# Four stacked layers on one core: index loads for two windows at once, an earlier reciprocal, later pieces of sample 1, and a column difference on VectorE

## The chip, the cores and the metric

The kernel runs on one core of a Trainium2 chip. The time is device microseconds (us) of one execution, the median of the runs shown. The engines are named as the profile names them: PE (TensorE's matmuls; PEld its weight loads), DVE (VectorE), ACT (ScalarE), POOL (GpSimd) and SP (SyncE, which here only issues DMAs). PSUM is the memory that matmuls write; SBUF is the one that the other engines work in.

## What is computed

A batch `x` of 8 samples, 128 channels, 56 x 56 pixels, float32, goes through four residual layers; each adds its result to a group-normalised input's branch:

```python
x = x + L0(_gn(x))   # windowed attention: 7x7 windows of 8x8 pixels, each attends to the 4 windows
                     # with the largest logits of window means; plus a depthwise 3x3 on v, then W_o
x = x + L1(_gn(x))   # batch norm, a tanhshrink projection, a recurrent net over 3136 pixels, projection
x = x + L2(_gn(x))   # a masked 3x3 convolution and a masked 1x1
x = x + L3(_gn(x))   # conv3x3, bn, relu, conv3x3, bn, + residual, relu
```

The part of layer 0 that matters here, and layer 3:

```python
logit = einsum('npc,nqc->npq', q_win * SCALE, k_win)
topk_logit, r_idx = top_k(logit, 4)
kv_sel = vmap(lambda kvn, idx: kvn[idx])(kv_pix, r_idx)          # 4 windows of keys and values
attn = softmax(einsum('bmqc,bmkc->bmqk', q_h * SCALE, k_sel))    # 8 heads
o = einsum('bmqk,bmkc->bmqc', attn, v_sel)

out = relu(bn1(conv3x3(x, w1)))
out = relu(bn2(conv3x3(out, w2)) + residual)
```

## The kernel before

X stays in SBUF. The order of PE, ACT, DVE and POOL in layers 0 and 3 is the order in which the program text issues them (`manual_schedule`); SP's queue runs in its own order of issue. Waits are put in between engines where data needs them.

**Layer 0** handles 8 x 49 windows as 196 pairs. In the loop over `p`, the pair `p + 1` gets its scores, row maxima (DVE, `nmax`), exponentials with their sums (ACT, `e`, `den`) and half its transposes, while the pair `p` finishes: second half of the transposes, copies to SBUF (`eT`, DVE and ACT in turn), the products with the values (`po`), the division. The names in the strings `SHORT` and `LONGER` (L762 to L765) are the order of one turn of the loop.

- `gather(W)` (L467): POOL reads the 4 indices of a window into registers (`chosen`, L457, a register load of four numbers at L460), copies the four key windows (L474, `ks`) and masks the queries (L476, `qm`). It is called two pairs ahead, from `ahead(p)` (L767).
- `fetch(W)` (L482): SP reads the same 4 indices into its own registers and issues 4 DMAs (L487, 32 KB each) of value windows from `vpix` in DRAM into `vs`, of which six buffers rotate, one per window.
- `divisors(p)` (L521): a DVE reciprocal of the exponentials' sums (L524, `rden`) and two POOL multiplications that spread it (L527, `rc`); `turn_divisors` transposes `rc` on PE (L556, `po`) in the next turn, ahead of the products with the values in PE's queue (L566).
- `light` is a small statistics or routing job (a matmul and its small follow-up): `mean`, `var`, `means`, `route`, once per sample. The follow-up of `var` (L235, samples 1 to 7) is three DVE operations and then twelve small POOL operations in a row (L246 to L249, three rounds of Newton's method for an inverse root).
- The work of later samples (normalising, keys, image rows, pixel rows, queries, depthwise, projection) is cut into pieces with a turn from which each is ready and one by which it is due; a planner (from L715 on) gives each turn up to two pieces and one light job. For sample 1 the statistics are due by turns 0 and 1, and the pieces of normalising stand at turns 2, 4, 6, 8, 10, 12, 15.

**Layer 1** (about 1345 to 2870 us) and **layer 2** (to about 3068 us) aren't touched.

**Layer 3** is two 3x3 convolutions of each sample, each as four blocks of 14 rows. Six column combinations per block (`column_sums`, L1403) go into the padded inputs `va` (first convolution) and `vb` (second), PE multiplies (`products`, L1440), and DVE combines (`outputs`, L1451). A `column_sums` has three parts: `outer` (two subtractions: `ce`, L1415, and `fg`, L1416, both on POOL save for two early `ce`), `inner` (DVE: `ab`, L1420; its sum and difference at L1421 and L1422 on DVE for `vb`, on POOL for `va`), and `ends` (DVE: L1426 to L1428, which read `ce` and `fg`). `block` puts these between its own steps: `outer` of the block before comes right after the copy on ACT, `inner` for `vb` just before the last operation of `outputs` (L1464), and for `va` behind it, after the two residual operations (L1558, L1559); `ends` follow. Thus POOL's queue holds, per block of the first convolution, `ce`, `fg`; and per block of the second one, `ce`, `fg` and then the sum and difference of `va`.

Of the kernel before, what the change touches and what calls it, by code (L numbers as in the profile page):

```python
# [10 lines left out]
F32 = mybir.dt.float32  # L11
# [3 lines left out]
ALU = mybir.AluOpType  # L15
# [3 lines left out]
P = 128  # L19
# [3 lines left out]
NW = 7  # L23
WS = 8
NWIN = NW * NW
WPX = WS * WS
# [18 lines left out]
def conv_stack_kernel(ctx: ExitStack, tc: tile.TileContext, a: dict, out: bass.AP):  # L45
# [80 lines left out]
    with ExitStack() as l0:  # L126
# [329 lines left out]

        def chosen(W, engine):  # L457

            b, w = divmod(W, NWIN)
            _, idx = nc.values_load_multi_w_load_instructions(  # L460
                selrs[b][0:1, w * TOPK : (w + 1) * TOPK], engines=[engine],
                min_val=0, max_val=NWIN - 1,
                skip_runtime_bounds_check_because="indices of maxima over 49 values, clamped to 48",
            )
            return idx

        def gather(W):  # L467


            b, w = divmod(W, NWIN)  # L470
            i, j = divmod(w, NW)
            kw = win.tile([P, TOPK, WPX], F32, name=f"ks_{W}", tag="ks")
            for t, at in enumerate(chosen(W, mybir.EngineType.Pool)):
                nc.gpsimd.tensor_copy(kw[:, t : t + 1, :], ks[b][:, bass.ds(at, 1), :])  # L474
            qm = win.tile([P, 2, WPX], F32, name=f"qm_{W}", tag="qm")
            nc.gpsimd.tensor_tensor(  # L476
                qm, qs[b, i][:, j : j + 1, :].broadcast_to((P, 2, WPX)),
                hmask.rearrange("p (h o) -> p h o", o=1).broadcast_to((P, 2, WPX)), ALU.mult,
            )
            wins[W] = dict(kw=kw.rearrange("p t x -> p (t x)"), qm=qm)  # L480

        def fetch(W):  # L482

            vw = wins[W]["vw"] = win.tile([P, 2, P], F32, name=f"vs_{W}", tag="vs", bufs=6)
            for t, at in enumerate(chosen(W, mybir.EngineType.SP)):
                h = (t % 2) * WPX
                nc.sync.dma_start(  # L487
                    vw[h : h + WPX, t // 2, :],
                    vpix[W // NWIN % 2][bass.ds(at, 1)].rearrange("o x c -> (o x) c"),
                )  # L490

        def scores(p):

# [194 lines left out]
        for b in range(1, B):  # L688

            at = [FIRST + 1] * NBLK if b == 1 else [pair_of(b - 2, 0) + i for i in range(NBLK)]  # L690
            if b > 1:
                for i in range(NBLK):
                    hook(max(at[i] - 8, FIRST + i // 2), lambda b=b, i=i: load_x(b, i, i + 1, nc.gpsimd))
            for i in range(4 * (b == 1), NBLK):
                hook(at[i], lambda b=b, i=i: once(measure, b)[0](i))
            job(at[-1] + 1, at[-1] + (1 if b == 1 else 5), lambda b=b: once(measure, b)[1], False, LIGHT, ("mean", b))
            job(at[-1] + 2, at[-1] + (2 if b == 1 else 9), lambda b=b: once(measure, b)[2], False, LIGHT,
                ("var", b), [("mean", b)])

            at = [pair_of(b - 1, i * NW) - 6 for i in range(NBLK)]  # L700
            if b == 1:
                at = [max(t, 2 + 2 * i) for i, t in enumerate(at)]
            due = pair_of(b, 0) - 3
            for i in range(NBLK):
                hook(at[i], lambda b=b, i=i: once(preparation, b)[0](i))
                job(at[i] + 1, due, lambda b=b, i=i: once(preparation, b)[1][i])
                job(at[i] + 1, due if i < 2 else pair_of(b, i * NW) - 10,
                    lambda b=b, i=i: once(preparation, b)[2][i], True)
                job(at[min(i + 1, NBLK - 1)] + 1, due - 1, lambda b=b, i=i: once(preparation, b)[3][i])
            job(at[-1] + 1, due - 2, lambda b=b: once(preparation, b)[4], False, LIGHT, ("means", b))  # L710
            job(at[-1] + 2, due - 1, lambda b=b: once(preparation, b)[5], False, LIGHT, None, [("means", b)])
# [43 lines left out]
        for k, (name, n) in enumerate(VECTORS):  # L755
# [4 lines left out]


        SHORT = """scores gather turn1 max0 max1 one turned old0 max2 exp00 exp01 old1 exp10 values end1 exp11 max3  # L762
            two exp02 exp03 exp12 exp13 hooks turn0 spread new1 end2 new0 tails light divisors divide"""
        LONGER = """scores gather turn1 max0 max1 exp00 old1 one end1 max2 max3 exp01 two old0 values turned exp02
            exp03 exp10 exp11 exp12 exp13 hooks turn0 spread new1 end2 new0 tails light divisors divide"""  # L765

        def ahead(p):  # L767
            if p + 2 < END:
                for W in (2 * p + 4, 2 * p + 5):
                    gather(W)  # L770
                for W in (2 * p + 4, 2 * p + 5) if p > FIRST + 1 else ():
                    fetch(W)
            for f in later:
                f()
            later.clear()
            for W in (2 * p - 2, 2 * p - 1):
                b, w = divmod(W, NWIN)
                if 0 <= b < B and w % NW == NW - 1:
                    join(b, w // NW)
# [13 lines left out]
        for p in range(FIRST, END + 6):  # L793
            now, then = 0 <= p < END, 0 <= p + 1 < END
            one, two, light = (t and t[3]() for t in plan[p])
            E, O = 2 * p + 2, 2 * p + 1
            acts = {
                "gather": lambda: ahead(p), "hooks": lambda: every(hooks.get(p, ())), "tails": rest,
            }
            if then:  # L800
                acts.update(scores=lambda: scores(p + 1), divisors=lambda: divisors(p + 1), turn0=lambda: turn(E),
                            new0=lambda: turned(E, 0), new1=lambda: turned(E, 1))
                for g in range(4):
                    acts[f"max{g}"] = lambda g=g: maxima(p + 1, g)
# [12 lines left out]
            for name in (LONGER if plan[p][1] and (not plan[p][0] or plan[p][1][5] == LONG) else SHORT).split():  # L817
                if name in acts:
                    acts[name]()
            for W in range(4) if p == FIRST + 1 else ():  # L820
                fetch(W)
        for f in later:
            f()
# [249 lines left out]
    def convolutions(held=None):  # L1073

        with ExitStack() as l2:
# [327 lines left out]
            def column_sums(v, lo, img, name, last=nc.vector, quick=False):  # L1403

                n = img.shape[2]
                at = [v[:, k].rearrange("p y x -> p (y x)")[:, lo * H4 : lo * H4 + n] for k in range(6)]
                ab, ce, fg = (
                    blk.tile([P, 2, size], F32, name=f"{k}_{name}", tag=k, bufs=2 - (k == "ab"))[:, :, :n]
                    for k in ("ab", "ce", "fg")
                )  # L1410
                other = nc.vector if quick else nc.gpsimd

                def outer():

                    other.tensor_tensor(ce, img[:, 3:5], img[:, 1:3], ALU.subtract)  # L1415
                    nc.gpsimd.tensor_tensor(fg, img[:, 0:4:3], img[:, 2:6:3], ALU.subtract)  # L1416

                def inner():

                    nc.vector.scalar_tensor_tensor(ab, img[:, 1:3], -4.0, img[:, 3:5], ALU.mult, ALU.add)  # L1420
# [395 lines left out]
```

## Time and profile before

| what | us |
|---|---|
| median of three runs (lowest, highest) | 3516.68 (3515.09, 3519.86) |
| the profiled execution's own time | 3514.11 |
| its span, first to last instruction | 3512.3 |
| PE busy in the span | 3396.8 (97%) |
| DVE, ACT, POOL busy | 1943.8, 1772.1, 1399.9 |
| layer 0, last products with values | ends at about 1337 |
| layer 3, first matmul to end of span | 3070.9 to 3512.3 |

The busy shares are averages over four layers with different limits. In layer 0 and layer 3 the waits of PE and the order of the queues of SP, DVE and POOL say more than the shares. TensorE's clock is granted in full nearly all the time; the profile records it as 0.992 over the span, and the stretches at one half are short (3.41 us or a multiple).

### The profile page before, as it was taken

The page shows a single profiled execution, that of the slowest core. Times are in us where ns is not written, and L with a number is a line of the kernel's source. Part 1 is how long each engine was busy: PE and PEld are TensorE (multiplying, and loading weights), DVE is VectorE, ACT ScalarE, POOL GpSimd, SP SyncE. Part 2 cuts the span into 40 slices and gives each one's busy share as a digit, 9 for nine tenths or more (in the row PEclk, how much of TensorE's full clock was granted, in tenths as well). Part 3 has the DMA queues.
Part 4 walks back from the last instruction along what each step waited for, and adds up shares of the span by engine and source line. Part 5 has one row for each costly group of instructions (what it writes and reads, how often), then busy time and mean ns, then how long its engine had stood idle before and what let it go on. Part 6 is the DMA issues. An engine that isn't in the chain of part 4 may idle for free.

```text
span 3512.3 us, 87799 instructions
## 1 busy us (share of the span) xinstructions
PE 3396.8 (97%) x30960; PEld 2810.4 (80%) x30960; DVE 1943.8 (55%) x4107; ACT 1772.1 (50%) x5322; POOL 1399.9 (40%) x3774
## 2 busy tenths in 40 slices
PE   8999999999999989999999999999999999999998
PEld 5666666666666668999999999999999973389888
DVE  7887888888888764222111111111112237699999
ACT  6787888888888873222222222222211124445554
POOL 4777776777766662111111111111100026534443
PEclk9999999999999999999999999999999999999999
DMA  5444444444444432111000000000002236500001
GB/s 154 124 121 117 122 121 117 125 120 126 109 107 117 122 87 66 46 46 49 14 1 1 1 1 1 1 1 1 1 26 58 58 85 181 134 19 33 24 38 38
DMA packets 197807, 238.19 MB, mean 68 GB/s; under 512 B 42752, under 2 KB 150400, under 8 KB 197360
## 3 DMA queue, kind: packets, MB, share of 16 engines
q0 software_dynamic: 34624, 117.03, 12.6%
q1 hardware_dynamic: 161760, 114.92, 11.6%
q8 instruction: 250, 4.10, 0.5%
q14 instruction: 197, 1.61, 0.2%
q10 hardware_dynamic: 976, 0.53, 0.1%
HBM read 133.80 MB, written 67.56 MB: 57 GB/s over the span
## 4 chain that ended last, share of the span: by engine, by line
PE 74%; DVE 14%; issue 4%; DMA 4%; ACT 2%; SPq 1%; POOL 1%; POOLq 0%; DVEq 0%; ACTq 0%
PE ps L968 33%; PE pt L539 7%; PE po L1003 5%; PE s L504 5%; PE plep L410 4%; PE pc L1194 4%; PE po L566 3%; DMA vs<-vpix 3%; PE pc3b L1440 3%; PE pi L943 2%; DVE nmax L512 2%; SPq L487 1%; PE pc L1202 1%; PE pvt L296 1%; DVE eT L544 1%
## 5 line engine op out<-in xcount | busy, mean ns | idle before, releaser
L968 PE MATMUL ps<-hs,w_gates 128*128 128x136 f32 x7680 | 932.9, 280 | 0.4 <-DVE gk L980 0.4
L968 PEld LDWEIGHTS ps<-hs,w_gates 128*128 128x128 f32 x7680 | 911.1, 190 | 8.6 <-issue 0.6
L516 ACT ACTIVATE e<-s,nmax 128x256 f32<-128x256 f32 x1568 | 728.4, 483 | 197.4 <-DVE nmax L512 197.4
L991 ACT ACTIVATE hs<-ps,bg 128x136 f32<-128x136 f32 x744 | 237.3, 370 | 933.6 <-PE ps L968 926.1
L946 DVE SCALAR_TENSOR_TENSOR inp<-pi,bine,th 128x272 f32<-128x272 f32 x186 | 84.7, 497 | 889.2 <-ACT th L945 889.2
L512 DVE TENSOR_REDUCE nmax<-s 128x2 f32<-128x512 f32 x784 | 507.2, 681 | 42.0 <-PE s L504 41.2
L539 PEld LDWEIGHTS pt<-ident,e 128*128 128x128 f32 x3136 | 349.3, 142 | 128.1 <-issue 48.7
L932 POOL TENSOR_TENSOR xn<-X,ctr 128x136 f32<-128x136 f32 (+1 forms) x186 | 96.3, 537 | 875.7 <-PE pi L943 871.8
L539 PE MATMUL pt<-ident,e 128*128 128x128 f32 x3136 | 429.5, 279 | 5.0 <-ACT e L516 3.1
L968 PEld LDWEIGHTS ps<-inp,w_gates 128*128 128x128 f32 x2976 | 370.2, 190 | 13.5 <-PE pi L943 1.1
L968 PE MATMUL ps<-inp,w_gates 128*128 128x136 f32 x2976 | 375.3, 279 | 0.8 <-DVE inp L946 0.8
L544 DVE COPY eT<-pt 128x512 f32<-128x512 f32 x392 | 267.3, 682 | 146.8 <-PE pt L539 146.8
L516 ACT ACTIVATION_READ_ACCUMULATOR e<-s,nmax 128x1 f32 x1568 | 331.7, 212 | 0.0
L474 POOL COPY ks<-kT 128x64 f32 x1568 | 297.6, 233 | 27.8 <-ACT vrow L302 24.7
L527 POOL TENSOR_TENSOR rc<-rden,own 128x128 f32<-128x128 f32 x392 | 147.7, 396 | 352.1 <-DVE rden L524 198.1
L566 PE MATMUL po<-eT,vs 128*32 128x128 f32 x6272 | 225.8, 278 | 32.2 <-DMA vs<-vpix 28.2
L544 ACT COPY eT<-pt 128x512 f32<-128x512 f32 x392 | 231.3, 590 | 39.4 <-PE pt L539 39.2
L566 PEld LDWEIGHTS po<-eT,vs 128*32 128x32 f32 x6272 | 160.6, 110 | 104.3 <-issue 47.6
L504 PE MATMUL s<-ks,qm 32*128 32x256 f32 x3136 | 243.4, 401 | 0.0
L1440 PE MATMUL pc3a<-va,u_w1c_t 128*128 128x196 f32 x1152 | 203.5, 335 | 13.9 <-DVE d_pc3a L1457 5.8
L1440 PE MATMUL pc3b<-vb,u_w2c_t 128*128 128x196 f32 x1152 | 199.4, 335 | 14.3 <-DVE vb L1421 14.3
L1440 PEld LDWEIGHTS pc3a<-va,u_w1c_t 128*128 128x128 f32 x1152 | 194.6, 193 | 22.0 <-POOL fg_pc3a L1416 5.4
(283 smaller groups left out, 4739.2 us busy)
## 6 DMA issues: line engine op xcount, KB each, us to landing
vs<-vpix SPq DMA_DIRECT2D x1568, 32.0 KB, 2.5
v<-vimg POOLq DMA_DIRECT2D x56, 290.0 KB, 4.0
v<-vimg POOLq DMA_DIRECT2D x56, 289.5 KB, 4.9
v<-vimg POOLq DMA_DIRECT2D x56, 289.0 KB, 5.7
kept<-gk SPq DMA_DIRECT2D x56, 272.0 KB, 2.1
g<-kept SPq DMA_DIRECT2D x56, 272.0 KB, 2.7
xkeep<-X POOLq DMA_DIRECT2D x56, 224.0 KB, 2.4
vimg<-vrow POOLq DMA_DIRECT2D x54, 232.0 KB, 2.9
```

Of the source, the lines that this page charges most:

```text
L474: nc.gpsimd.tensor_copy(kw[:, t : t + 1, :], ks[b][:, bass.ds(at, 1), :])
L504: nc.tensor.matmul(s_["s"][g][:, o, :], w["qm"][h].rearrange("p h x -> p (h x)"), w["kw"][h], start=True, stop=True,)
L512: nc.vector.tensor_reduce(s_["nmax"][:, g, :], s_["s"][g], AX.X, ALU.max, negate=True)
L516: nc.scalar.activation(wins[2 * p + o]["e"][:, g, :], s_["s"][g][:, o, :], AF.Exp, bias=s_["nmax"][:, g, o : o + 1], accum_out=s_["den"][: ...
L527: nc.gpsimd.tensor_tensor(pairs[p]["r"][:, o], rden[:, o].rearrange("p (g c) -> p g c", c=1).broadcast_to((P, 4, CL)), own.rearrange("p (g ...
L539: nc.tensor.transpose(s_["pt"][c][:, g, :], s_["e"][:, g, c * P : (c + 1) * P], ident)
L544: (nc.scalar.copy if c else nc.vector.tensor_copy)(s_["eT"][c], s_["pt"][c])
L566: nc.tensor.matmul(po[ch, o, 0], s_["vw"][:, c, ch], s_["eT"][c][:, g, :], start=(c == 1), stop=(c == 0),)
L968: nc.tensor.matmul(ps[f][:, i], w, src, start=(i == 0 and k == 0 and h != fresh), stop=(k == KH - 1 if h else k == KI - 1 and (s < WARM or ...
L991: nc.scalar.activation(hs[f][:, s % 2, i], ps[f][:, i], AF.Tanh, bias=bg[:, m : m + 1])
L1003: nc.tensor.matmul(po, wout[:, k, :], hs[k // 2][:, :, k % 2], start=(k == 0), stop=(k == KH - 1))
L1440: nc.tensor.matmul(bank[:, half].rearrange("p (y x) -> p y x", x=H4), u[:, dy, k, :], v[:, k, i * RB + dy : i * RB + dy + RB, :], start=(d ...
```

## The change

Four edits. Index loads: `chosen` reads the 8 indices of two windows with one register load (two loads where the pair crosses a sample), on POOL and on SP; `gather` and `fetch` handle both windows of a pair in the same order of copies and DMAs as before. Divisors: `divisors` stands ahead of `light` in both orders. Sample 1: its statistics are due two turns later (the planner moves them from turns 0 and 1 to turns 2 and 3), and its normalising stands at turns 4, 5, 7, 8, 10, 11, 15. Layer 3: `fg` leaves `outer` on POOL and becomes the first operation of `inner` on DVE.

```diff
         def chosen(W, engine):
-            b, w = divmod(W, NWIN)
-            _, idx = nc.values_load_multi_w_load_instructions(
-                selrs[b][0:1, w * TOPK : (w + 1) * TOPK], engines=[engine],
...
-            return idx
+            idx = []
+            while len(idx) < 2 * TOPK:
+                b, w = divmod(W + len(idx) // TOPK, NWIN)
+                n = min(NWIN - w, 2 - len(idx) // TOPK)
+                idx += nc.values_load_multi_w_load_instructions(
+                    selrs[b][0:1, w * TOPK : (w + n) * TOPK], engines=[engine],
...
+                )[1]
+            return idx[:TOPK], idx[TOPK:]
         def gather(W):
-            for t, at in enumerate(chosen(W, mybir.EngineType.Pool)):
...
+            for W, idx in zip((W, W + 1), chosen(W, mybir.EngineType.Pool)):
...
         def fetch(W):
-            vw = wins[W]["vw"] = win.tile([P, 2, P], F32, name=f"vs_{W}", tag="vs", bufs=6)
-            for t, at in enumerate(chosen(W, mybir.EngineType.SP)):
...
+            for W, idx in zip((W, W + 1), chosen(W, mybir.EngineType.SP)):
+                vw = wins[W]["vw"] = win.tile([P, 2, P], F32, name=f"vs_{W}", tag="vs", bufs=6)
+                for t, at in enumerate(idx):
...
-            job(at[-1] + 1, at[-1] + (1 if b == 1 else 5), ... ("mean", b))
-            job(at[-1] + 2, at[-1] + (2 if b == 1 else 9), ... ("var", b), [("mean", b)])
+            job(at[-1] + 1, at[-1] + (3 if b == 1 else 5), ... ("mean", b))
+            job(at[-1] + 2, at[-1] + (4 if b == 1 else 9), ... ("var", b), [("mean", b)])
...
-                at = [max(t, 2 + 2 * i) for i, t in enumerate(at)]
+                at = [max(t, 4 + 3 * i // 2) for i, t in enumerate(at)]
...
-            two exp02 exp03 exp12 exp13 hooks turn0 spread new1 end2 new0 tails light divisors divide"""
+            two exp02 exp03 exp12 exp13 hooks turn0 spread new1 end2 new0 tails divisors light divide"""
-            exp03 exp10 exp11 exp12 exp13 hooks turn0 spread new1 end2 new0 tails light divisors divide"""
+            exp03 exp10 exp11 exp12 exp13 hooks turn0 spread new1 end2 new0 tails divisors light divide"""
...
                 def outer():
                     other.tensor_tensor(ce, img[:, 3:5], img[:, 1:3], ALU.subtract)
-                    nc.gpsimd.tensor_tensor(fg, img[:, 0:4:3], img[:, 2:6:3], ALU.subtract)
                 def inner():
+                    nc.vector.tensor_tensor(fg, img[:, 0:4:3], img[:, 2:6:3], ALU.subtract)
                     nc.vector.scalar_tensor_tensor(ab, img[:, 1:3], -4.0, img[:, 3:5], ALU.mult, ALU.add)
```

More of the change, by code (lines that the diff above doesn't have):

```diff
@@ L457, in chosen @@
         def chosen(W, engine):
-            b, w = divmod(W, NWIN)
-            _, idx = nc.values_load_multi_w_load_instructions(
-                selrs[b][0:1, w * TOPK : (w + 1) * TOPK], engines=[engine],
-                min_val=0, max_val=NWIN - 1,
-                skip_runtime_bounds_check_because="indices of maxima over 49 values, clamped to 48",
-            )
-            return idx
-        def gather(W):
-            b, w = divmod(W, NWIN)
-            i, j = divmod(w, NW)
-            kw = win.tile([P, TOPK, WPX], F32, name=f"ks_{W}", tag="ks")
-            for t, at in enumerate(chosen(W, mybir.EngineType.Pool)):
[L474 to L480, printed above, removed]
@@ L482, in fetch @@
-        def fetch(W):
-            vw = wins[W]["vw"] = win.tile([P, 2, P], F32, name=f"vs_{W}", tag="vs", bufs=6)
-            for t, at in enumerate(chosen(W, mybir.EngineType.SP)):
[L486 to L490, printed above, removed]
+            idx = []
[4 more added lines that the diff above has]
+                    selrs[b][0:1, w * TOPK : (w + n) * TOPK], engines=[engine],
+                    min_val=0, max_val=NWIN - 1,
+                    skip_runtime_bounds_check_because="indices of maxima over 49 values, clamped to 48",
+                )[1]
@@ new lines, in chosen @@
+            return idx[:TOPK], idx[TOPK:]
+        def gather(W):
+            for W, idx in zip((W, W + 1), chosen(W, mybir.EngineType.Pool)):
+                b, w = divmod(W, NWIN)
+                i, j = divmod(w, NW)
+                kw = win.tile([P, TOPK, WPX], F32, name=f"ks_{W}", tag="ks")
+                for t, at in enumerate(idx):
+                    nc.gpsimd.tensor_copy(kw[:, t : t + 1, :], ks[b][:, bass.ds(at, 1), :])
+                qm = win.tile([P, 2, WPX], F32, name=f"qm_{W}", tag="qm")
+                nc.gpsimd.tensor_tensor(
+                    qm, qs[b, i][:, j : j + 1, :].broadcast_to((P, 2, WPX)),
+                    hmask.rearrange("p (h o) -> p h o", o=1).broadcast_to((P, 2, WPX)), ALU.mult,
+                )
+                wins[W] = dict(kw=kw.rearrange("p t x -> p (t x)"), qm=qm)
@@ L492, in scores @@
+        def fetch(W):
+            for W, idx in zip((W, W + 1), chosen(W, mybir.EngineType.SP)):
+                vw = wins[W]["vw"] = win.tile([P, 2, P], F32, name=f"vs_{W}", tag="vs", bufs=6)
+                for t, at in enumerate(idx):
+                    h = (t % 2) * WPX
+                    nc.sync.dma_start(
+                        vw[h : h + WPX, t // 2, :],
+                        vpix[W // NWIN % 2][bass.ds(at, 1)].rearrange("o x c -> (o x) c"),
+                    )
         def scores(p):
@@ L695, in conv_stack_kernel @@
                 hook(at[i], lambda b=b, i=i: once(measure, b)[0](i))
-            job(at[-1] + 1, at[-1] + (1 if b == 1 else 5), lambda b=b: once(measure, b)[1], False, LIGHT, ("mean", b))
-            job(at[-1] + 2, at[-1] + (2 if b == 1 else 9), lambda b=b: once(measure, b)[2], False, LIGHT,
+            job(at[-1] + 1, at[-1] + (3 if b == 1 else 5), lambda b=b: once(measure, b)[1], False, LIGHT, ("mean", b))
+            job(at[-1] + 2, at[-1] + (4 if b == 1 else 9), lambda b=b: once(measure, b)[2], False, LIGHT,
                 ("var", b), [("mean", b)])
@@ L762, in conv_stack_kernel @@
         SHORT = """scores gather turn1 max0 max1 one turned old0 max2 exp00 exp01 old1 exp10 values end1 exp11 max3
-            two exp02 exp03 exp12 exp13 hooks turn0 spread new1 end2 new0 tails light divisors divide"""
+            two exp02 exp03 exp12 exp13 hooks turn0 spread new1 end2 new0 tails divisors light divide"""
         LONGER = """scores gather turn1 max0 max1 exp00 old1 one end1 max2 max3 exp01 two old0 values turned exp02
-            exp03 exp10 exp11 exp12 exp13 hooks turn0 spread new1 end2 new0 tails light divisors divide"""
+            exp03 exp10 exp11 exp12 exp13 hooks turn0 spread new1 end2 new0 tails divisors light divide"""
         def ahead(p):
             if p + 2 < END:
[L769 to L772, printed above, removed]
+                gather(2 * p + 4)
+                if p > FIRST + 1:
+                    fetch(2 * p + 4)
             for f in later:
@@ L819, in conv_stack_kernel @@
                     acts[name]()
-            for W in range(4) if p == FIRST + 1 else ():
+            for W in (0, 2) if p == FIRST + 1 else ():
                 fetch(W)
```

## The prediction

> **What bounds the kernel now.** I read the page for the stages, the table by windows for the limits of layers 0 and 3 (layers 1 and 2 aren't touched), the list of waits for what PE waits for in layer 0, the chain of waits around the longest of these, and the timelines of DVE and POOL in layer 3.
>
> A row of the list of waits (who for whom: us in total, times, longest), and the end of the answer for line 527 alone:
>
> ```profile
> PE po L566 <- DMA vs<-vpix: 28.2, 25, 2.9
> ```
> ```profile
> who waited for it (us, times):
>   PEld po L556: 12.0, 13
>   PE po L556: 8.3, 5
> ```
>
> In layer 0 PE is mostly 95 to 99% busy, and these two waits are of the kind that nothing hides: PE, in order, stands before the products with the values until SP's DMAs have landed (28.2 us), and before the transposes of `rc` (8.3 us at 5 places). The chain at one of the five shows why:
>
> ```profile
> 597.66 0.16 DVE r L242
> 597.82 0.07 issue
> 597.89 0.20 POOL nr L246
> ...
> 600.89 0.19 POOL r L249
> 601.08 0.21 POOLq L460
> 601.29 0.15 POOL rc L527
> 601.45 0.04 issue
> 601.49 0.33 PE po L556
> ```
>
> Twelve small POOL operations of `var` run from 597.89 to 601.08, only then comes `rc`, and PE starts `po` 1.81 us late. It is charged twice: the table by windows has the granted clock at 0.50 from 603.26 to 606.67.
>
> SP's timeline shows no gap:
>
> ```profile
> 619.85 30.59 SPq L487 DMA_DIRECT2D vs<-vpix  x38
> ```
>
> 38 issues in 30.59 us are merged into one piece. From the starts of single instructions in the trace: issues stand 0.65 us apart, but 1.07 us across a register load, and a pair (8 issues, 2 loads) takes at least 6.05 us. From 36 to 1330 us SP takes 6.62 us per pair, PE 6.66: SP is a second bound as tight as PE. So its DMAs come late wherever PE has an easy stretch: 19 of the 25 waits lie after 900 us.
>
> Layer 3 (us, busy time of PE, PEld, DVE, ACT, POOL; clock, DMA):
>
> ```profile
> 3200.00:3300.00 100.00, 93.49 (x541) 91.08 (x542) 99.48 (x212) 55.12 (x65) 42.77 (x45) 0.98 0.08 30
> ```
>
> DVE is the bound here, not PE. But some of DVE's time is standing still:
>
> ```profile
> 3266.69 0.49 DVE L1459 TENSOR_TENSOR w_pc3a<-s_pc3a 128x196 f32<-128x196 f32 x1
> 3267.11 1.17 DVE L1460 SCALAR_TENSOR_TENSOR w_pc3a<-d_pc3a 128x196 f32<-128x196 f32 x1
> 3268.20 0.35 DVE L1461 SCALAR_TENSOR_TENSOR y_pc3a<-s_pc3a 128x196 f32<-128x196 f32 x1
> ```
> ```profile
> 3265.95 1.02 POOL L1415 TENSOR_TENSOR ce_pc3a<-edge 128x392 f32<-128x392 f32 x1 [3.59 <-ACT edge L1302]
> 3266.92 1.14 POOL L1416 TENSOR_TENSOR fg_pc3a<-edge 128x392 f32<-128x392 f32 x1
> ```
>
> L1460 takes 1.17 us while `fg` runs on POOL, its twin L1461 right after it 0.35. Operations that read one operand from PSUM (L1456, L1457, L1464) keep their 0.55 beside the same POOL work.
>
> **The change part by part.** I sum against the profile's span, 3512.3 us; the median of the runs is 4.4 us above it.
>
> *Divisors before light.* DVE's reciprocal needs only ACT's sums. In `var` turns `rc` then stands ahead of the twelve operations (3.2 us). The five waits are 1.81, 1.43, 1.81, 1.42 and 1.81 us, 8.3 together; two of them (279, 603 us) are followed by a window of 3.41 us at half clock, worth up to 1.7 each. Bounds: gain 11.7 to 0. From the first score of a pair to that of the next (starts in the trace), the five take 9.95, 7.80, 9.89, 7.80 and 8.32 us; their likes 6.6 (6.8 with a depthwise piece): 10.2 us above. What is late next: the twelve still stand before `gather` of the same turn, which ends near 603.7 as before, while the scores that read it would now start near 603.2. I leave 0.7 for that: **-9.5**.
>
> *One load for two windows.* 192 register loads go on SP and as many on POOL. On SP one takes 0.297 us, with its gaps 0.36 (1.07 - 0.65, less 0.05 for a semaphore step that stays). What a load of 8 costs isn't in the trace. From below: a load of one number takes 0.307 on POOL and 0.393 on SP, four take 0.318 and 0.297, so more numbers cost nothing seen, and 8 cost 0.30. From above: twice 0.297 plus nothing saved but gaps of 0.06. I take the first, as one against four numbers is the nearest row. SP then needs some 0.34 us less per pair, 66 us over layer 0, and runs ahead up to its six buffers; POOL's loads lie under its copies. The waits after 200 us (25.9 us) end. Not all of it is gained, since ACT needs 6.18 us per pair (the shortest pitch that recurs): summed over those pairs, the pitch above that of equal pairs without a wait is 12.7 us, 5.5 of it in the last sample. Bounds: 0 to -29 (25.9, and 1.7 for each of two half-clock windows at 1231 and 1279 us). I take **-11**.
>
> The Trainium skill's "Runtime: NRT & Kernel Launch" (section Instruction fetch mechanics) says that such a load costs about 200 ns for each register, even in bulk. By it a load of 8 would cost as much as two of 4, and SP would gain next to nothing. The trace doesn't agree in size: 0.297 for four is 74 ns each. It is the reason for a rival below.
>
> *Sample 1.* The same pieces, moved by two turns. `mean` and `var` leave turns 0 and 1, where PE waited 1.3 and 1.6 us for a PSUM bank behind ACT's `vrow`, for turns 2 and 3, which have a depthwise and an image piece and so the same kind of wait; two normalising pieces (0.7 + 0.6 us of DVE each) come later. **-0.5**, bounds -4 and +3.
>
> *Layer 3.* 64 subtractions go from POOL to DVE. Cost there: `ab` and `d` of the same 392 columns step 0.47 us, so 64 x 0.47 = 30.1. Relief, by rows of equal shape:
>
> ```profile
> L1460 DVE SCALAR_TENSOR_TENSOR w_pc3a<-d_pc3a 128x196 f32<-128x196 f32 x32 | 22.6, 708 | 0.0
> ...
> L1460 DVE SCALAR_TENSOR_TENSOR w_pc3b<-d_pc3b 128x196 f32<-128x196 f32 x32 | 17.0, 530 | 0.0
> ...
> L1461 DVE SCALAR_TENSOR_TENSOR y_pc3a<-s_pc3a 128x196 f32<-128x196 f32 x32 | 11.2, 349 | 0.0
> ...
> L1420 DVE SCALAR_TENSOR_TENSOR ab_va<-pad 128x420 f32<-128x420 f32 x7 | 10.3, 1472 | 0.0
> ```
>
> 32 x (708 - 350) + 32 x (530 - 350) ns = 17.2 us behind `fg_pc3a`; 7 x (1472 - 600) = 6.1 behind `fg_va` of a sample's first block (600 from 561 for 392 columns); five stretched operations at 3068 to 3088 us, 3.6. Sum 26.9. The other `fg` run beside `s` and `d`, which read PSUM, and cost DVE nothing now. DVE: +3.2. It isn't the bound in the last four blocks, and in the first sample only partly: **+2**. `fg` needs ACT's border columns too, which POOL finds ready two operations sooner today; behind it wait `ab` and POOL's sums of `va`. Bounds: -4 (only the relief that starts the layer earlier counts) to +30 (no relief).
>
> Sum: -9.5 - 11 - 0.5 + 2 = **-19**; span 3493.3, median 3497.7.
>
> **The rivals.**
> - *The load is priced by the number.* Eight would take 2 x 0.297 us, SP's pair stay at 6.05 less gaps, and the waits for values stay: -9.5 - 0.5 + 2 = -8, 3508.7. For it: SP never pauses, so its own time decides. Against it: one number costs as much as four. The Trainium skill's page named above would have it so.
> - *`gather` becomes the wait.* With `rc` early, scores would wait for `ks` behind the twelve operations. For it: 603.7 against 603.2 at 603 us. Against it: half a microsecond, in five turns. If it gave back 1.5 us in each: -19 + 7.5 = -11.5, 3505.2.
> - *Slower: the stall in layer 3 only moves.* POOL's `ce` and its sums of `va` (1.0, 0.5 us) could slide under DVE's two-SBUF operations as `fg` did, so that the 30.1 us come without relief. For it: DVE is 99% busy, all goes to the end. Against it: `ce` is released by ACT after the same DVE operation as before. -21 + 30.1 = +9, 3525.8. It decides from 28 us of the 30 on (28 - 21 is 0.2%).
> - *The waits convert whole.* PE catches up nothing today: -11.7 - 25.9 - 0.5 + 2 = -36, 3480.6.
> - *Nothing arrives*: both layers are held by another limit (ACT's 6.18 per pair, DVE), 3516.
>
> **How the numbers follow.** Chances: my forecast 0.58, load 0.12, `gather` 0.08, slower 0.08, whole 0.09, nothing 0.05. A difference under 0.2% (7 us) can't be told from none. Faster: 0.56 of mine, half of the load's (3508.7 lies at the edge, 3509.6), 0.07, 0.09: 0.78. Slower 0.08. The rest, 0.14, is the same. The range, 3483 to 3512, leaves out the slower case, the last one and a part of the whole one.
>
> **What would show it.** SP: a pair in 5.7 us, pieces with waits in between, and `po <- DMA vs` near zero after 200 us; right if register loads of 8 take about 0.3 us, wrong at 0.6. `po <- POOL rc` gone, pairs at 279 and 603 us near 6.6, full clock there; wrong if `s <- POOL ks` or `qm` appears. Layer 3: `w` L1460 at 0.35, `fg` on DVE at 0.55, the first matmul about 1 us sooner after DVE's first `ab`, a sample's period 53.6 us within 0.5; wrong if L1459, L1428 or L1421 grow by what L1460 lost.

## The result, and the profile after

| | before, us | changed, us | ratio, 95% interval |
|---|---|---|---|
| first measurement | 3517.64 (4 runs) | 3496.45 (4 runs, 3493.56 to 3502.57) | 0.9943 [0.9928, 0.9959] |
| second | 3507.7 (9 runs) | 3493.24 (5 runs) | 0.9958 [0.9944, 0.9972] |

The forecast was 3497.7; the gain is 21 us in the first measurement, 15 in the second. The median of the kernel before differs by 10 us between series of runs, so below only ratios to the kernel before of the same series, on the same chip, are compared. The profile shown here is of the slowest of the first four executions (3502.57 us, span 3500.2). In the changed kernel the line numbers of layer 0 are 4 to 6 higher from the load on: the load of the indices is L464, `ks` L479, `qm` L481, the value DMAs L493, `rc` L533, `po` L562 (transposes of `rc`) and L572 (products with the values).

The waits of PE (who for whom: us in total, times, longest):

```profile
PE po L572 <- DMA vs<-vpix: 12.2, 8, 2.8
PE py L436 <- POOL lep L428: 3.7, 3, 1.2
PE s L510 <- POOL qm L481: 1.3, 5, 0.4
```

The waits for values went from 28.2 us at 25 places to 12.2 at 8; in the trace two of these lie before 50 us, none between 50 and 1170, and six in the last sample. The 8.3 us for `rc` are gone, and among the waits that the list of before did not show are PE's `py` for POOL's `lep` (the join of attention and depthwise branch) and scores for the masked queries, which the prediction had named as a sign against it.

The register loads (minimum, median, maximum in ns), SP's of before first, then all of L464:

```profile
L460 SPq TENSOR_LOAD <-selr x392: 293/297/1480, 30.9 to 1330.7; - x196
...
L464 POOLq TENSOR_LOAD <-selr x200: 316/566/1369, 23.2 to 1307.5; - x100
L464 SPq TENSOR_LOAD <-selr x200: 297/524/2359, 29.1 to 1313.3; - x100
```

Half as many loads as before, but a load of eight takes 0.524 us on SP where one of four took 0.297. The chain of waits at the place that the prediction showed (start us, us, what):

```profile
595.68 0.10 DVE rden L530
...
595.92 0.76 POOL rc L533 x2
596.68 0.16 POOL nr L246
...
599.37 0.19 POOL nr L248
...
600.41 0.12 POOL ks L479
...
602.20 0.36 POOL qm L481
602.56 0.58 POOL xkeep L442
...
603.17 1.15 POOL lep L427
...
604.40 1.14 POOL lep L428
...
605.58 1.02 PE py L436 x2
```

`rc` is now ready at 596.68, ahead of the twelve operations; before it was at 601.45, behind them (the turn itself lies some 1.6 us earlier in this trace). These still run to 599.6; behind them stand the gather, and behind the gather the two `lep` operations, 2.3 us, that PE now waits for. Layer 3 over a stretch like the one shown of before (us, then busy time of PE, PEld, DVE, ACT, POOL; clock, DMA):

```profile
3188.00:3288.00 100.00, 93.20 (x547) 91.89 (x546) 99.48 (x228) 56.61 (x68) 26.65 (x32) 0.98 0.08 31
```

DVE is busy for the same 99.48 us in 100, with 228 operations in place of 212, and POOL for 26.7 in place of 42.8: the work moved and the stalls it caused on DVE went.

Where the gain lies, by starts in the two traces: pair 0 to pair 18 of layer 0, 125.4 us before and 129.8 after; 18 to 26, 51.6 and 51.7; 26 to 173, 974.6 and 958.3; 173 to 195, 146.3 and 147.6; layer 3 from DVE's first operation to the end, 443.9 and 442.1. Almost all of it is in layer 0 from pair 26 to 173. Layers 1 and 2 moved with it. The spans of these two traces differ by 12.1 us, less than the medians of the runs do.

### The profile page after: what moved, and what is told of

It is laid out like the page before. It is cut to its first block, busy times and chain, and to the rows that moved or that the text cites. A ratio compares the mean times of both kernels' runs of the same rounds, so it can differ in the third digit from the quotient of the medians.

```text
span 3500.2 us, 87334 instructions
## 1 busy us (share of the span) xinstructions
PE 3396.0 (97%) x30960; PEld 2810.8 (80%) x30960; DVE 1944.5 (56%) x4171; ACT 1771.9 (51%) x5322; POOL 1334.8 (38%) x3710
## 3 DMA queue, kind: packets, MB, share of 16 engines
q1 hardware_dynamic: 161760, 114.92, 11.7%
## 4 chain that ended last, share of the span: by engine, by line
PE 73%; DVE 18%; issue 4%; ACT 3%; POOL 1%; DMA 1%; SPq 1%; POOLq 0%; DVEq 0%; ACTq 0%
PE ps L973 33%; PE pt L545 8%; PE s L510 5%; PE po L1008 5%; PE pc L1199 4%; PE plep L410 4%; PE po L572 3%; DVE nmax L518 3%; PE pi L948 2%; ACT e L522 2%; DVE eT L550 1%; PE pc L1207 1%; PE pvt L296 1%; PE pc3b L1445 1%; PE py L436 1%
## 5 line engine op out<-in xcount | busy, mean ns | idle before, releaser
L479 POOL COPY ks<-kT 128x64 f32 x1568 | 298.2, 235 | 44.4 <-issue 27.1
L533 POOL TENSOR_TENSOR rc<-rden,own 128x128 f32<-128x128 f32 x392 | 147.7, 396 | 333.9 <-DVE rden L530 174.7
L572 PE MATMUL po<-eT,vs 128*32 128x128 f32 x6272 | 222.3, 276 | 19.8 <-DMA vs<-vpix 12.2
L572 PEld LDWEIGHTS po<-eT,vs 128*32 128x32 f32 x6272 | 159.9, 109 | 89.5 <-issue 49.1
L1445 PEld LDWEIGHTS pc3b<-vb,u_w2c_t 128*128 128x128 f32 x1152 | 198.8, 196 | 22.2 <-DVE vb L1426 22.0
```

The lines of the kernel that those rows point to most:

```text
L533: nc.gpsimd.tensor_tensor(pairs[p]["r"][:, o], rden[:, o].rearrange("p (g c) -> p g c", c=1).broadcast_to((P, 4, CL)), own.rearrange("p (g ...
L572: nc.tensor.matmul(po[ch, o, 0], s_["vw"][:, c, ch], s_["eT"][c][:, g, :], start=(c == 1), stop=(c == 0),)
L1445: nc.tensor.matmul(bank[:, half].rearrange("p (y x) -> p y x", x=H4), u[:, dy, k, :], v[:, k, i * RB + dy : i * RB + dy + RB, :], start=(d ...
```

## The experiments: each part alone

The four parts were run in one series, each alone in the kernel before (before: 3512.64 us, 29 runs). The edits are the hunks of the diff above.

```diff
# e1_loads: the hunks of chosen, gather, fetch, ahead
# e2_divisors
-... new0 tails light divisors divide"""
+... new0 tails divisors light divide"""
# e3_sample1: due turns of mean and var, turns of the pieces
-max(t, 2 + 2 * i)
+max(t, 4 + 3 * i // 2)
# e4_layer3
-outer: nc.gpsimd.tensor_tensor(fg, ...)
+inner: nc.vector.tensor_tensor(fg, ...)
```

> Only the loads of eight indices. By the prediction: a load of 8 costs 0.30 us, SP's shortest pair falls from 6.05 to about 5.7 us, the waits of PE for values after 200 us end, and the time falls by 11 us (0 to 29). By the theory after the trace of the changed kernel: a load of 8 takes 0.52 us on SP, a pair saves only 0.13 us (25 us over layer 0), which still ends the waits from 50 to 1160 us but not those of the last sample; the time falls by 10 to 13 us. By the rival (load priced by the number in full): SP saves nothing, the waits stay at 28 us in total, the time changes by less than 3 us.

> Only the divisors ahead of the light pieces. By the prediction: the five waits of PE for rc (8.3 us) and two windows at half clock go, the time falls by 9.5 us. By the theory after the trace of the changed kernel: the waits move behind the twelve operations of Newton's rounds, to the join's matmuls and to the masked queries of the next pair, which then takes 7.2 to 8.0 us in place of 6.2 to 6.6; the time falls by 2 to 4 us. By the rival that gather takes the whole wait: change within 1 us, and the waits of scores for qm or ks total more than 5 us.

> Only sample 1's pieces two turns later. By the prediction: -0.5 us (-4 to +3). By the theory after the trace of the changed kernel: the waits for ACT's vrow move from turns 0 and 1 to 2 and 3 and pairs 13 and 17 wait for late pieces of x (8.4 in place of 6.8 us), so the start of pair 18 against that of pair 0 is 2 to 4 us later and the time rises by 1 to 4 us.

> Only the outer column difference of layer 3 on VectorE. By the prediction: +2 us (-4 to +30): 30.1 us more work on DVE, 26.9 less standing still. By the theory after the trace of the changed kernel: the w operations on L1460 of before fall to 0.35 us and those of 1.47 us to 0.6, the time changes by -1 to -2 us. By the rival that the stall only moves: +28 us or so, with ce or the sums of va beside operations that take over 1 us.

| part alone | ratio, 95% interval | us | predicted, us |
|---|---|---|---|
| loads | 0.9941 [0.9924, 0.9957] | -20.7 (-26.7 to -15.1) | -11 |
| divisors | 1.0003 [0.9994, 1.0013] | +1.1 (-2.1 to +4.6) | -9.5 |
| sample 1 | 1.0008 [0.9998, 1.0019] | +2.8 (-0.7 to +6.7) | -0.5 |
| layer 3 | 0.9985 [0.9976, 0.9995] | -5.3 (-8.4 to -1.8) | +2 |

(us: ratio less one, times 3512.6.) The loads alone give what the whole change gives, and the four parts add up to -22.1.

**Loads.** The list of waits of this kernel (line numbers of the changed kernel), the rows for values and for `rc`:

```profile
PE po L562 <- POOL rc L533: 8.3, 5, 1.8
PE po L572 <- DMA vs<-vpix: 7.8, 6, 2.4
```

`rc` is untouched, and the waits for values are down by 20.4 us, from 28.2 to 7.8. That this is the 20.7 us of the medians is partly luck: the spans of the two traces differ by 16.8, and the traces of three other kernels whose loads were not touched have 16.7 to 20.1 us of these waits at times within 6 us of before's. Part by part it is clearer. In pairs 26 to 173 the waits go from 12.4 us to none, a window of 3.41 us at half clock goes too, and the stretch is 14.2 us shorter (974.6 to 960.4): there the waits came back whole. In pairs 173 to 195 they fall by 5.8 us, the stretch by 1.5.

The gain was nearly twice the 10 to 13 us that the later theory expected, although SP saves less than the prediction had it. The edit also halves POOL's loads, and that half was not run alone; but before's list has no wait of PE for `ks` or `qm` that it could have ended. What SP's saving buys is a lead. From the trace: from the issue of a pair's last value transfer to the first product that reads that window, median and minimum in us:

| pairs | before | loads alone | changed |
|---|---|---|---|
| 26 to 60 | 7.3, 5.1 | 11.1, 9.2 | 11.8, 9.9 |
| 60 to 100 | 8.3, 5.4 | 10.3, 7.6 | 10.9, 8.9 |
| 100 to 140 | 7.1, 4.2 | 10.6, 9.0 | 10.7, 8.1 |
| 140 to 173 | 4.9, 3.3 | 10.4, 6.5 | 7.7, 5.1 |
| 173 to 195 | 4.3, 2.0 | 5.3, 2.2 | 4.7, 2.2 |

Before, the lead falls to 4.2 us and less; with loads of eight it stays above 7.5 up to pair 140, and shrinks again in the last sample. Traces differ, so the rows have to be read over all kernels here: the median of the first row is 6.1 to 11.7 with loads of four and 7.3 to 13.0 with longer ones, which tells nothing; that of the third is 5.8 to 7.4 against 8.9 to 11.5, of the fourth 4.3 to 6.0 against 7.7 to 12.8. In the last sample it varies from 4.7 to 8.3 with the longer loads, and the waits there with it (12.2 us to none).

How long a transfer can take is seen at the one long wait in the second measurement of the changed kernel; its chain, and POOL's timeline just before:

```profile
1210.45 0.35 issue
1210.80 7.05 DMA vs<-vpix
1217.85 0.14 issue
1217.98 1.08 PE po L572 x16
```
```profile
1209.64 1.70 POOL L397 DMA_DIRECT2D v<-vimg  x3
```

A value transfer lands 2.5 us after its issue (median of the 197 landings that before's trace shows, of 1568 transfers), but this one took 7.05. The eight longest of these waits in four kernels with loads of eight were followed back in the same way: the transfers landed 5.5 to 7.05 us after issue, and each had been issued 1.2 to 2.6 us after the first of three image DMAs of 290 KB on POOL's queue. At such places a lead of 6 us is not enough. The places are not chosen by the waits alone: of the 197 landings of before, the 21 whose issue came 1 to 3 us after such a first image DMA took 4.7 to 6.3 us (median 5.4), the other 176 a median of 2.4.

**Divisors.** Against the other theories: the rows of the list that changed (line numbers of before; there, `po` for `e` was 2.0 us).

```profile
PE po L566 <- DMA vs<-vpix: 26.6, 29, 2.4
PE po L566 <- ACT e L516: 5.9, 5, 2.1
PE py L436 <- POOL lep L428: 3.7, 3, 1.2
```

The 8.3 us for `rc` are gone, but `py` waits 3.7 and the products wait 3.9 us more for ACT's `e`; the waits for values stay. Pairs 26 to 140, which hold all five places, take 754.2 us before and 754.1 here (the other kernels with loads of four and an unchanged SP vary from 751.3 to 758.2). Nothing was gained: part of the wait moved behind Newton's rounds, and the rest came back at other places. Neither the 9.5 us of the prediction nor the 2 to 4 of the later theory came. That SP is as tight as PE is not the reason: beside loads of eight the same edit gains no more than 0.5 us of this stretch (next section).

**Sample 1.** Pairs 13 and 17 take 8.4 and 8.5 us, as in the changed kernel, where before has 6.8; from pair 0 to pair 18 it takes 130.2 us in place of 125.4 (but pairs 0 and 1 alone vary from 14.9 to 21.4 among all the kernels here, so that this sum says little). The total agrees with the theory after the trace, but its interval reaches below zero; the cause is settled further below.

**Layer 3.** DVE's rows of this kernel (busy us, mean ns of one); `fg` is L1418, the other lines have the numbers of before:

```profile
L1418 DVE TENSOR_TENSOR fg_pc3a<-edge 128x392 f32<-128x392 f32 x32 | 17.7, 553 | 0.0
...
L1460 DVE SCALAR_TENSOR_TENSOR w_pc3b<-d_pc3b 128x196 f32<-128x196 f32 x32 | 11.2, 350 | 0.0
...
L1460 DVE SCALAR_TENSOR_TENSOR w_pc3a<-d_pc3a 128x196 f32<-128x196 f32 x32 | 11.2, 349 | 0.0
...
L1420 DVE SCALAR_TENSOR_TENSOR ab_va<-pad 128x420 f32<-128x420 f32 x7 | 4.1, 583 | 0.0
...
L1428 DVE SCALAR_TENSOR_TENSOR va<-ce_va,fg_va 128x210 f32<-128x210 f32 x7 | 2.6, 365 | 0.0
```

Both `w` are at 0.35 (0.708 and 0.530 before) and `ab_va` at 0.58 (1.472), as predicted. The last row is one that the prediction had missed; `va` of 210 columns before:

```profile
L1428 DVE SCALAR_TENSOR_TENSOR va<-ce_va,fg_va 128x210 f32<-128x210 f32 x7 | 8.3, 1192 | 0.0
```

That is 5.8 us more of relief. These rows (without `fg`) fall by 29.1 us together, against the 30.1 that `fg` adds, and the layer starts 0.88 us sooner: first matmul 2.54 us after DVE's first operation in all six kernels without this edit (to 0.01), 1.66 in all eight with it. DVE's busy time in the layer falls from 432.7 to 429.5 us, where the prediction had 3.2 more. From DVE's first operation to the end the six take 443.0 to 444.9 us (mean 444.0), the eight 440.9 to 444.2 (mean 442.0). The traces put the gain at 2 us; the times, at 1.8 to 8.4. The stall did not move. The Trainium skill's "SBUF — State Buffer" (section SBUF: two separate sides) says that a DVE operation with two SBUF inputs and a GpSimd operation that reads SBUF hold a shared pair of ports in turn, for the whole instruction; these rows agree (0.35 with POOL's `fg` gone, 1.17 beside it).

## The experiments: parts together, and what stands behind the twelve operations

In a second series (before: 3511.07 us, 11 runs): loads and layer 3; these and the divisors; and these with the twelve operations of `var` taken apart.

```diff
# c1_loads_layer3, c2_loads_divisors_layer3: the hunks above
# c3_newton_spread: c2, and in var's follow-up
-                for _ in range(3):
-                    ... four operations of one Newton round
+                def once_more():
+                    ... four operations of one Newton round
+                if b > 1:
+                    rounds.extend([once_more] * 3)
+                else:
+                    for _ in range(3):
+                        once_more()
# and in ahead(p), behind the joins
+            for f in rounds[:1]:
+                f()
+            del rounds[:1]
```

> The changed kernel without the divisors and without sample 1: loads and layer 3 only. If the divisors' gain in the changed kernel is what its trace shows (3 us) and sample 1 costs 3 us, this one takes what the changed kernel takes, 21 us below before (ratio 0.994). By the prediction's terms (divisors 9.5, sample 1 0.5) it would be 10 us slower than the changed kernel (ratio 0.997).

> The changed kernel without sample 1. If sample 1 costs 3 us, this one is 24 us below before (ratio 0.993), pair 18 starts some 126 us after pair 0, as in before, and not 130. If the later start in the changed kernel is by chance, the ratio is 0.994 and the start varies. Against the kernel with loads and layer 3 alone: -3 us if SP's slack turns the divisors into a gain, 0 if the five waits only move.

> The one before this (loads, divisors, layer 3), and the twelve operations behind the reciprocal square root are no longer issued in one turn ahead of the gather, but four per turn, behind the joins, over three turns (samples 2 and 3). Theory: those twelve are what the wait moved behind, so the next pair's 8.0 us (36+1, 85+1, 134+1) and 7.2 us (62, 111) fall to 6.2 to 6.6, the wait of py for the join ends, and the time falls by 5 to 7 us more (ratio 0.991). Rival: the join and the reciprocal themselves, not the twelve, hold the turn: pairs stay at 8.0 and the time the same within 2 us.

| kernel | us | ratio, 95% interval | pairs 36, 37 | 61, 62 | 26 to 140 |
|---|---|---|---|---|---|
| before (first profile) | | | 9.95, 6.19 | 7.80, 6.61 | 754.1 |
| loads, layer 3 | 3495.21 | 0.9954 [0.9936, 0.9971] | 8.32, 6.19 | 7.80, 6.61 | 747.3 |
| and divisors | 3492.12 | 0.9948 [0.9930, 0.9965] | 6.66, 8.04 | 6.19, 7.19 | 746.8 |
| and Newton spread | 3488.33 | 0.9935 [0.9918, 0.9953] | 6.53, 6.19 | 6.19, 6.80 | 740.3 |

The intervals of neighbouring rows overlap (and that of loads and layer 3 overlaps that of the loads alone, 0.9941, in the first series), so for single steps the traces decide. By the times, neither ratio that the first expectation weighs, 0.994 or 0.997, is ruled out; the 0.991 of the third is.

The divisors take 1.7 us from pair 36 and put 1.9 on pair 37, and likewise at the other places; over pairs 26 to 140 that is worth 0.5 us, so the five waits only moved. Only when Newton's rounds are spread do both pairs of each couple come down, and the stretch falls by another 6.5 us. Of the waits of `py` for `lep` and of scores for `qm` nothing is left in the list of that kernel. So the twelve operations, and not the order of `rc` alone, held the turn: the two steps together are worth 7.0 us of pairs 26 to 140, where the prediction had 9.5 for the first. Spreading the rounds without the earlier `rc` was not run.

## The experiments: SP's own bound

The kernel before, with a second reading of the indices on SP (same series).

```diff
+            chosen(W, mybir.EngineType.SP)
             for t, at in enumerate(chosen(W, mybir.EngineType.SP)):
```

> The kernel before, with SP reading each window's four indices twice (a second load whose result isn't used): 0.30 to 0.36 us more on SP per window, 0.6 to 0.7 per pair. If SP is a second bound as tight as PE (6.62 us per pair used, 6.05 the shortest), its pair rises to 6.65 at the shortest and to 7.1 to 7.3 with its stalls, the waits for values grow to several hundred, and the time rises by 80 to 130 us. If the waits come from something else (the transfers' own time, the six buffers), the time rises by less than 20.

Measured 3552.61 us, ratio 1.0115 [1.0091, 1.0138]: 40 us slower (32 to 48), between the two theories. What this kernel's trace shows of L460, and its waits for values:

```profile
L460 SPq EVENT_SEMAPHORE  x392: 17/17/17, 27.4 to 1363.5; - x196
L460 SPq TENSOR_LOAD <-selr x392: 293/298/1258, 31.8 to 1367.1; - x196
```
```profile
PE po L567 <- DMA vs<-vpix: 40.8, 30, 6.8
```

The second load isn't there: as nothing reads it, building the program left it out, and one semaphore step per window stayed. Such a step costs 0.07 us (from the issue before the load to the one after it: 1.07 us with one step in between, as mostly in before, 1.14 with two, 1.21 with three, 1.28 with four), by estimate 27 us over 392 windows. SP also stops three times ahead of L460, for 3.6, 5.4 and 3.5 us, each time for the landing of the index transfer (L362) that it had issued shortly before; before's trace has no stop over 1.5 us in layer 0's loop. So the kernel does not measure what it was made for; but some 40 us more of SP's time, and of no other engine's, cost 40 us, about one for one, and the theory that SP is no bound (under 20 us) falls.

In a third series (before: 3507.7 us, 9 runs), beside the changed kernel once more, four windows' indices in one load of 16 on SP, in the kernel with the spread rounds:

```diff
+                if W not in kept:
+                    n = min(4, NWIN - w)
+                    idx = nc.values_load_multi_w_load_instructions(
+                        selrs[b][0:1, w * TOPK : (w + n) * TOPK], engines=[mybir.EngineType.SP], ...
```

> The kernel with the spread Newton rounds, and SP loads the indices of up to four windows (16 numbers) at once, for two pairs. If a load costs 0.07 us and 0.057 more per number (four 0.297, eight 0.524), 16 take 0.98 us, SP saves less than 0.1 us per pair and the time stays the same within 3 us. If the price flattens (0.6 to 0.7 for 16), SP saves 0.2 per pair more and the shortest pair falls below 5.8 us.

3484.37 us, ratio 0.9931 [0.9915, 0.9946], not to be told from loads of eight (0.9935, in the second series); pairs 26 to 140 take 740.2 us, as there. The load's row:

```profile
L501 SPq TENSOR_LOAD <-selr x104: 296/972/2782, 29.8 to 1301.5; - x104
```

0.972 us for 16, where the straight line through four and eight gives 0.98: the price is 0.07 us and 0.056 per number.

## The experiments: sample 1 and the last sample

> The changed kernel once more, for a narrower interval beside the parts: 20 us below before (ratio 0.994). Pairs 13 and 17 take 8.4 us each as in the two traces with sample 1's edit so far, where the eight traces without it have 6.8: a cost of 3.3 us that stays if sample 1's pieces are its cause, and that differs from run to run if the order of transfers at the start is.

Pairs 13 and 17 again take 8.41 and 8.48 us. The planner's table, worked out from the program text, shows why: with the pieces of sample 1 two turns later, 12 are waiting at turns 12 and 16 (7 and 11 before), and above 11 the planner puts one more piece beside the depthwise piece there. The kernel before with just that:

```diff
-                one, two = one if len(ready) > MANY else None, long
+                one, two = one if len(ready) > MANY or p in (12, 16) else None, long
```

> The kernel before, with one piece more beside the depthwise piece in turns 12 and 16, as sample 1's edit makes the planner do (more than 11 pieces are then waiting), and nothing else. Theory: that is the cost of sample 1's edit. Pairs 13 and 17 take 8.4 us in place of 6.8, the turns that lose the piece can't fall below ACT's 6.18, so pair 18 starts 2 to 3 us later against pair 0 (127 to 129 us in place of 124 to 126) and the time rises by 1 to 3 us. Rival: the later normalising pieces of sample 1 hold pairs 13 and 17; then they stay at 6.8 here.

The time can't tell (3517.73 against 3515.66 us, ratio 1.0005 [0.9994, 1.0016]), the trace can. Pair times in us:

| pair | 9 | 10 | 11 | 12 | 13 | 14 | 15 | 16 | 17 | sum |
|---|---|---|---|---|---|---|---|---|---|---|
| before | 7.12 | 6.61 | 6.58 | 6.47 | 6.80 | 6.18 | 6.30 | 6.18 | 6.80 | 59.0 |
| this kernel | 7.13 | 6.61 | 6.60 | 6.47 | 8.41 | 6.29 | 6.19 | 6.19 | 8.48 | 62.4 |
| changed | 7.44 | 6.64 | 6.89 | 6.48 | 8.40 | 6.29 | 6.19 | 6.19 | 8.48 | 63.0 |

The two long pairs are there without any piece of sample 1 being later, and the pairs that lost a piece stay at ACT's 6.18. At these two places the depthwise matmuls wait for the piece beside them; two rows of this kernel's answer for L410 (PE and PEld sat idle until, us, times):

```profile
  DVE q L384: 2.4, 2
  DVE X L441: 2.3, 2
```

Neither row is there in the answer for before. So sample 1's edit costs some 3.3 us in pairs 9 to 17; in pairs 2 to 8 (49.9 to 52.0 us in the three traces with it, 48.1 to 50.9 in the eleven without) a cost can't be told from what these vary by.

Last, the decoder's gate weights moved from SP's queue to POOL's, in the kernel with the spread rounds:

```diff
-            nc.sync.dma_start(weights[0], a["w_hh_t"]...
+            nc.gpsimd.dma_start(weights[0], a["w_hh_t"]...
# and the same for weights[1], [2] and [3]
```

> The kernel with the spread Newton rounds, and the decoder's four gate weights loaded by POOL's queue and not by SP's (their transfers start at about 1165 us). If these transfers are what puts SP behind in the last sample, PE's waits for values after 1160 us (5 to 12 us in the kernels with loads of eight) end and the time falls by 3 to 5 us more (ratio 0.990). If SP is late there for another reason, the waits of over 2 us stay and the time is the same within 2 us, or later by the issues on POOL.

3479.37 us, ratio 0.9918 [0.9905, 0.9932], the lowest of all. But the waits that it was to end are still there:

```profile
PE po L578 <- DMA vs<-vpix: 4.0, 5, 1.6
```

Two of 1.6 us lie at 1249 and 1295 us; their transfers landed 6.0 us after issue, each issued 1.2 us after the first of POOL's three image DMAs. The gate weights are not their cause. They are not sufficient for such waits either: with them on SP's queue, the trace of loads, divisors and layer 3 has no wait for values after 50 us, and the second one of the changed kernel has one, of 2.6. The interval overlaps that of the kernel without this edit, so whether it adds anything isn't shown. That the three edits together (loads, divisors with spread rounds, layer 3; without sample 1) beat the changed kernel is: 0.9918 [0.9905, 0.9932] against 0.9958 [0.9944, 0.9972] on one chip, with the gate weights' edit included.

## Why the prediction came out

The total was right (-19 forecast, -21 and -15 measured), but by luck: errors of the terms cancel.

- *Loads, -11; measured -20.7.* Two steps were off, in opposite directions. "The first" bound of the price (8 cost 0.30 us, as many as four) fails: 0.524. The row that it rested on, a load of one number, is a single execution per engine at the end of the kernel (L1592: 0.307 us on POOL and 0.393 on SP, and 0.477 to 0.807 on the other three), too little to say that more numbers cost nothing. SP's shortest pair that recurs went from 6.05 to 5.92 us and not to 5.7, so SP saves 0.13 us per pair (as do the loads: 2 x 0.297 less 0.524, and a gap of 0.06), 26 us in all, not 66. And "not all of it is gained" fails for pairs 26 to 173: there the waits that ended came back whole in the time, as the rival that lets the waits convert whole had it. A saving of 2% on the second bound was enough, since its lead adds up over many pairs. The waits after 200 us ended only up to 1170; in the last sample most traces still have them, and why the lead is short there isn't shown.
- *The rival "priced by the number".* Its price was nearer the truth than the one I took: eight cost 1.76 times four. Its consequence was wrong, as it let SP save nothing but gaps. The Trainium skill's "Runtime: NRT & Kernel Launch" (section Instruction fetch mechanics) gives some 200 ns per register, by which, as an estimate, eight would take 1.6 us. The traces show 0.524, and 0.056 per added number; that page speaks of loads from HBM, and these read SBUF, so its figure did not bear on them as the prediction took it.
- *Divisors, -9.5; measured +1.1 alone.* The waits for `rc` went as predicted. The two windows at half clock are gone too (the granted clock is 1.00 from 275 to 280 and from 600 to 605 us), but that need not be this edit's doing: in the kernel with loads and layer 3 alone, where the five waits stand, the clock is 1.00 there as well. The step "I leave 0.7 for that" failed: behind the twelve operations stand not only the scores' `ks` and `qm` but the joins, 2.3 us of POOL behind the gather, and `py` waits for them in PE's queue. That was the rival of `gather`, with a second victim and a larger price; that scores wait for `qm` was the prediction's own sign of being wrong here.
- *Sample 1, -0.5; measured +2.8 alone.* The waits behind ACT moved from turns 0 and 1 to 2 and 3 as said. What was missed is a rule of the planner: work that comes later piles up, and the turns with a depthwise piece then get another piece.
- *Layer 3, +2; measured -5.3 (-2 by the traces).* Mechanism right in each row named (L1460 now 0.35, `fg` 0.55, first matmul 0.9 us sooner); the relief was undersized, above all by the 210-column `va`. The rival of a stall that only moves did not occur.

## What to carry to other kernels

A second engine that is a few per cent from being the bound sets the time through its lead: compare its lead with the longest landing of its transfers and not with the median, and before a wait that ends is counted as gained, in full or in part, look for what holds next: the waits for values came back whole over most of layer 0, those for `rc` not at all. When an operation is pulled ahead of a block of small ones, list everything that still stands behind the block, to the end of the turn; spreading the block was worth more than jumping it. Where a planner fills turns by how much is waiting, compare its tables before and after, as a piece that is only moved can push another one into a full turn.

## What the runs showed of the hardware

- A register load from SBUF costs 0.07 us and 0.056 us for each number on SP (four 0.297, eight 0.524, sixteen 0.972); on POOL four cost 0.318 and eight 0.566. The one load of a single number on SP, at the kernel's end, took 0.393 and lies off this line.
- SP's DMA issues take 0.469 us (median), but 123 of the 1580 in layer 0 of before take over 0.6, with 74 us in excess in total. In 109 of these 123 a 16 KB packet of the queue named "instruction" (median 1.12 us) is under way within the first 0.47 us; so it is in 99 of the 1457 short ones. That is seen side by side and was not tested by an experiment; it is two thirds of what SP's register loads cost in before (392 x 0.297 = 116 us).
- A 32 KB transfer with a median landing of 2.5 us can take 5.5 to 7 us behind three transfers of 290 KB that another engine's queue issued 1 to 3 us earlier (in before 21 such took a median of 5.4). That is seen side by side as well; no run moved those three.
